# A sparse graph layer on one core: the first group's second tile of records found on chip, products turned, classes by limits

## The chip, the cores and the metric

The kernel runs on one core of a Trainium2 chip. Its time is the device time of one execution in microseconds (us), from the first to the last instruction with what the launch adds around it. The engines named below are TensorE (PE in the profile, its weight loads PEld), VectorE (DVE), ScalarE (ACT), GpSimd (POOL) and SyncE (SP), which issues the plain DMAs. Each engine works through its own queue in order.

## The reference

Sixteen graphs of 1024 nodes, 64 channels per node, and a dense adjacency matrix drawn so that a node has some four neighbours in the mean, very unevenly spread (the first nodes have many). Two layers follow each other. The first is a mean over neighbours; the second takes, per node and channel, quartiles over a thinned-out list of neighbours, and sends the result through a small network:

```python
# layer 0
h = jnp.maximum(_layernorm(x, axis=-1), 0.0)
deg = jnp.clip(jnp.sum(A, axis=2, keepdims=True), 1.0, None)
x = x + jnp.matmul(A / deg, h)
# layer 1, on h = relu(layernorm(x))
nb = (adj_ > 0) & (~eye)[None]
m = nb.sum(-1)
rank = jnp.cumsum(nb, axis=-1) - 1
skip = jnp.where(m > 10, (m + 1) // 2, 1)
removed = nb & do_dil[..., None] & ((rank + 1) % skip[..., None] == 0)
rem = removed | jnp.swapaxes(removed, 1, 2)
adj_d = jnp.where(rem, 0.0, adj_)
agg = 0.25 * q25 + 0.5 * q50 + 0.25 * q75      # over the valid neighbours, per channel
y = relu((h + agg) @ W1 + b1) @ W2 + b2
x = x + y * mask
```

## The kernel before, in words

The kernel replaces the dense second layer by lists. It has two stretches that overlap.

**Per graph** (16 times). SyncE loads the adjacency matrix in four pieces of 256 rows (tile `at`). For each 128 rows ScalarE writes the signs (`sg`) and, as an accumulated sum, the number of entries above zero (`total`); VectorE multiplies the signs by a descending ramp (`keyed`) and takes the top 8 of each of four interleaved segments (`listing`, 512 eight-way maxima in all), so that a node's neighbours are a record of up to 32 numbers, with the node's number and its mask as entries 33 and 34. TensorE transposes the blocks (`transposes`), ScalarE copies them to `att`, and `products` multiplies them by the normalized features `h0` with a column of ones, so that the sum over neighbours and the degree come out together. In the old form `h0` is the stationary operand and 512 columns of `att` move; the result has channels in its rows, so ScalarE copies it (`msg`) and TensorE transposes it back in four pieces. `channels` normalizes again and stores 1024 rows of 66 numbers to the group's table in DRAM (`tab`).

`endings` then sorts the graph's nodes by degree. It gives each node a class: the number of entries found, capped at 16, and above that one more for each of the limits 19, 22, 29, 39, 59, 79. A one-hot of 23 classes (`hot`), two matmuls against constants, and a running sum give each node its place `to` in the group's sorted order. GpSimd then scatters the node's row (table row, residual and record) to its place in DRAM (`srt`), by eight indirect DMAs a graph.

**Per group** (four groups of four graphs). The sorted nodes of a group fill 32 tiles of 128. Tile 0 holds the longest lists and is handled at the end as "long lists". Tile 1 has up to 15 neighbours, the rest fewer. `group` loads the records from `srt` (first tiles 0 and 1 alone as `recs0`, then all 32 as `recs`); for tile 0 it fetches the nodes' whole adjacency rows (`fetched`, an indirect DMA of 128 rows of 4 KB) and counts which entry the thinning takes out (`counted`); for tile 1 it does so from the list itself. The numbers of the removed neighbours (`drop`) are scattered into the group's table by two indirect DMAs, after which the neighbours' rows can be gathered: a `Job` per class of list length issues one indirect DMA per neighbour place and tile (`places`), sorts on VectorE with a network of minima and maxima, weighs on VectorE, sums and multiplies on TensorE, and scatters `y` to the output.

For group 0 the old kernel already knows tile 0's node numbers and masks before the sorted rows are in DRAM: after each of the first four graphs `hubs` compares `to` with 0 to 127 (a one-hot of 1024 elements per partition) and multiplies it with the nodes' numbers, the sum over four graphs being `hub_rows`; `begun_early` then does the fetch and the count. Tile 1's keys, both drops, and the gathers wait for `recs0` and `recs`.

**What sets the order.** All work is written as generators that a `Plan` interleaves: each `yield` names an engine and the earliest time; the plan keeps a clock per engine with a price per instruction, and always emits the entry with the lowest (time, rank). Low ranks go first: graph `b` has 10`b` plus a small number, `group` has -2000, row scatters 10`b` - 3000, the jobs 100`g` + `i`, and a job's sorting is moved ahead when GpSimd has fewer than 16 gathers ahead of it. VectorE and GpSimd keep this order exactly. Through the plan's wrapper nearly every instruction carries line 240 in the profile, so groups are told apart by their tiles. In the plan, an f32 matmul was priced so:

```python
time = 0.1 + math.prod(out.shape[1:]) * 0.88e-3
if op == "matmul" and rest[0].dtype == F32:
    time *= 2
```

The long lists' key (`long_lists`, four times) is written by the following operation, whose result is laid out in eight segments of 128:

```python
nc.vector.scalar_tensor_tensor(
    segs.rearrange("p s q -> p q s"), full.rearrange("p (q s) -> p q s", s=LSEG), 0.0,
    rev.rearrange("p (q s) -> p q s", s=LSEG), op0=OP.is_gt, op1=OP.mult,
)
```

Of the kernel before, what the change touches and what calls it, by code (L numbers as in the profile page):

```python
# [9 lines left out]
F32 = mybir.dt.float32  # L10
# [8 lines left out]
P = 128  # L19
# [9 lines left out]
NSEG = 4  # L29
STEPS = (16, 19, 22, 29, 39, 59, 79)  # L30
CLS = 15 + len(STEPS) + 1

# [15 lines left out]
MOST = 8  # L48

# [196 lines left out]
class Plan:  # L246
# [36 lines left out]
    def note(self, engine, op, args, kwargs):  # L283
# [22 lines left out]
        elif engine == "PE":  # L306
            time = 0.1 + math.prod(out.shape[1:]) * 0.88e-3
            if op == "matmul" and rest[0].dtype == F32:
                time *= 2
# [76 lines left out]
def list_path(ctx, tc, x, adj, nodemask, w1, b1, w2, b2, out, go):  # L386
# [36 lines left out]
    nc.vector.tensor_scalar(off_diag, diff, 0.0, None, op0=OP.not_equal)  # L423
    earlier = consts.tile([P, P], BF, name="earlier")
# [8 lines left out]
    nc.vector.tensor_copy(col_f, col)  # L433
    zero = consts.tile([P, 1], BF, name="zero")
# [6 lines left out]
    cls_i = grp.tile([P, N], I32, name="gat_rows", bufs=1)[:, :CLS * NT]  # L441
    cls_i = cls_i.rearrange("p (c t) -> p c t", t=NT)
    nc.gpsimd.iota(cls_i, pattern=[[-1, CLS], [0, NT]], base=CLS - 1, channel_multiplier=0)
    cls = consts.tile([P, CLS, NT], F32, name="cls")
    nc.vector.tensor_copy(cls, cls_i)
# [267 lines left out]
    def products(pool, now):  # L713


        for b, st in enumerate(batch):
            now[0] = b
            for hf in range(2):
                yield "PE", lambda: INF if st["copied"][hf] < 2 * BPH else max(
                    at(st["att"][hf]), known(st, "h0"), room("ps_small", 3)  # L720
                )
                po = new(ps_s, [P, HALF], F32, "ps_small", 3, users=1)
                for q in range(NT):
                    if q and q % 2 == 0:
                        yield "PE", always
                    nc.tensor.matmul(
                        po[:C + 1, :], st["h0"][:, q, :], st["att"][hf][:, q, :],
                        start=(q == 0), stop=(q == NT - 1),
                    )
                free(st["att"][hf])  # L730
                free(st["h0"])
                yield "ACT", lambda: max(at(po), room("msg", 2))
                msg = new(pool, [C + 1, HALF], F32, "msg", 2)
                nc.scalar.copy(msg, po[:C + 1, :])
                free(po)
                yield "PE", lambda: max(at(msg), room("ps_small", 3))
                pb = new(ps_s, [P, HALF], F32, "ps_small", 3, users=1)
                sums = pb[:, :BPH * (C + 1)].rearrange("p (k c) -> p k c", c=C + 1)
                for k in range(BPH):
                    nc.tensor.transpose(  # L740
                        sums[:, k, :], msg[:, k * P:(k + 1) * P], ident[:C + 1, :C + 1]
                    )
# [15 lines left out]
    def channels(pool, now):  # L758

        for b, st in enumerate(batch):  # L760
# [9 lines left out]
            st["normed"] = True  # L770

    def endings(pool, now):

        first = lambda rank: rank - 3000
        for b, st in enumerate(batch):
# [6 lines left out]
            for t in range(NT):  # L782
# [6 lines left out]
            found = new(pool, [P, NT, 8 * NSEG], BF, "found", 1)  # L789
            nc.vector.tensor_scalar(found, rec, 0.0, None, op0=OP.is_gt)  # L790
            d = new(tiny, [P, NT], F32, "d", 2)
            nc.vector.tensor_reduce(d, found, AX.X, OP.add)
            full = new(tiny, [P, NT], F32, "full", 2)
            nc.vector.tensor_reduce(
                full, found.rearrange("p t (s e) -> p t s e", e=8)[:, :, :, 7], AX.X, OP.max
            )
            nc.vector.scalar_tensor_tensor(d, full, float(STEPS[0]), d, op0=OP.mult, op1=OP.max)
            nc.vector.tensor_scalar(d, d, float(STEPS[0]), None, op0=OP.min)
            for s in STEPS[1:]:
                nc.vector.scalar_tensor_tensor(d, total, float(s), d, op0=OP.is_gt, op1=OP.add)  # L800
            free(rec)
            free(total)
            hot = new(tiny, [P, CLS, NT], BF, "hot", 2)
            nc.vector.tensor_tensor(
                hot, cls, d.unsqueeze(1).to_broadcast([P, CLS, NT]), OP.is_equal
            )
# [33 lines left out]
            if g == 0:  # L840
                plan.add(hubs(b, to), 10 * b + 8)
# [28 lines left out]
    class Job:  # L870
# [11 lines left out]
        def run(self):  # L882
# [14 lines left out]
            if short:  # L897
# [3 lines left out]
                if "S" not in share:  # L901
                    S = share["S"] = new(
                        pool, [P, mine_of(share), C], F32, "S", 4, users=share["users"]
                    )
                    nc.sync.dma_start(S, share["rows"][:, :, :C])
# [23 lines left out]
            yield from self.sort()  # L929

# [296 lines left out]
    hub_rows = consts.tile([P, 2], F32, name="hub_rows")  # L1227
    early = {}

    def hubs(b, to):  # L1230

        tof = new(tiny, [P, NT], F32, "tof", 2)
        yield "DVE", lambda: max(at(to), room("gfound", 1))
        nc.vector.tensor_copy(tof, to)
        where = new(grp, [P, N], HF, "gfound", 1).rearrange("p (t k) -> p t k", t=NT)
        nc.vector.tensor_tensor(
            where, col_f[:, :P].unsqueeze(1).to_broadcast([P, NT, P]),
            tof.unsqueeze(2).to_broadcast([P, NT, P]), OP.is_equal,
        )
        yield "PE", lambda: max(at(where), room("ps_small", 3))  # L1240
        ph = new(ps_s, [P, HALF], F32, "ps_small", 3, users=1)
        for t in range(NT):
            nc.tensor.matmul(
                ph[:, :2], where[:, t, :], marks[:, b, t, :], start=(t == 0), stop=(t == NT - 1)
            )
        yield "DVE", lambda: at(ph) + SLACK
        if b:
            nc.vector.tensor_tensor(hub_rows, hub_rows, ph[:, :2], OP.add)
        else:
            nc.vector.tensor_copy(hub_rows, ph[:, :2])  # L1250
# [628 lines left out]
```

## Time and profile before

| | us |
|---|---|
| median of 3 runs (lowest, highest) | 1414.26 (1410.16, 1416.34) |
| the profiled execution's own time | 1414.18 |
| its span, first to last instruction | 1412.4 |
| VectorE busy | 1228.7 (87%) |
| GpSimd busy | 963.8 (68%) |
| TensorE busy | 738.8 (52%) |
| ScalarE busy | 557.6 (39%) |
| GpSimd's first gather of neighbours / last gather | 194.84 / 1360.5 |
| mean granted TensorE clock | 0.711 |

A line in order of time reads: start, duration (both us), engine, line, operation, result <- operands with shapes, count, and in brackets the idle time of the engine just before it with what ended it; "issue" is idle time in which nothing that the profile shows was waited for. A line of a group by shape reads: result <- operands, shapes, count | total busy us, mean ns of one | idle us before, and what ended it. In the table of 40 slices each digit is the busy share of a slice in tenths. In the matmul rows an f32 product counts twice, since it is done in two passes, and a transpose once.

### The profile page before, as it was taken

How to read it: one execution, taken by the hardware profiler on the slowest of the kernel's cores; microseconds unless marked ns; L12 is line 12 of the kernel's file. 1: busy time of each engine (PE TensorE's matmuls, PEld its weight loads, DVE VectorE, ACT ScalarE, POOL GpSimd, SP SyncE). 2: the span in 40 equal slices, each digit the busy share in tenths (PEclk: the TensorE clock that was granted, in tenths of full speed). 3: DMA queues.
4: the chain of work that ended last, by engine and by line, in shares of the span. 5: the costliest groups of instructions: out<-in, count | busy, mean ns of one | idle time of the engine just before them, and what ended most of it. 6: DMA issues, size and time to landing. Idle time of an engine off the chain costs nothing.

```text
span 1412.4 us, 14420 instructions
## 1 busy us (share of the span) xinstructions
PE 738.8 (52%) x3203; PEld 458.2 (32%) x3203; DVE 1228.7 (87%) x4150; ACT 557.6 (39%) x1603; POOL 963.8 (68%) x1115
## 2 busy tenths in 40 slices
PE   4878726376677657839856652002002232337685
PEld 2434413243443335425442331001001121226455
DVE  6999898999888898998999668886998899998985
ACT  6889763765554356865653520000000110001010
POOL 0042347777775787776778877775877777787764
PEclk9999868687787868968966865555555555557566
DMA  5464582443444245545541324211111111111110
GB/s 174 156 195 163 182 228 76 133 154 90 124 107 136 69 119 170 150 142 148 158 125 46 85 46 84 73 44 46 32 25 24 25 34 26 25 28 40 25 25 16
DMA packets 133834, 132.31 MB, mean 94 GB/s; under 512 B 99444, under 2 KB 102132, under 8 KB 133620
## 3 DMA queue, kind: packets, MB, share of 16 engines
q1 hardware_dynamic: 102220, 91.13, 21.8%
q0 software_dynamic: 31520, 40.19, 11.7%
q8 instruction: 27, 0.44, 0.1%
q14 instruction: 67, 0.55, 0.1%
HBM read 111.76 MB, written 23.61 MB: 96 GB/s over the span
## 4 chain that ended last, share of the span: by engine, by line
DVE 46%; POOL 18%; issue 10%; PE 10%; DMA 9%; ACT 6%; SPq 0%; DVEq 0%; POOLq 0%; ACTq 0%
POOL places L240 14%; DVE places L240 8%; DVE rec L240 6%; DVE other L240 5%; PE ps_small L240 5%; PE pt L240 5%; DVE lplaces L240 4%; DVE sg L240 2%; DMA at<-in_adj_dram 2%; DMA places<-tab,idx 2%; DVE l0other L240 2%; ACT sg L240 2%; POOL srt L240 2%; DVE prod L240 2%; DVE lkey L240 1%
## 5 line engine op out<-in xcount | busy, mean ns | idle before, releaser
L240 POOL DMA_INDIRECT places<-tab,idx x372 | 375.8, 1010 | 121.2 <-issue 104.2
L240 PE MATMUL pt<-ident,prod 128*128 128x128 f32 (+1 forms) x736 | 152.2, 367 | 385.8 <-DVE prod L240 330.9
L240 PE MATMUL ps_small<-att,h 128*65 128x512 f32 x512 | 261.7, 662 | 77.3 <-ACT h L240 55.9
L240 PEld LDWEIGHTS pt<-ident,prod 128*128 128x128 f32 (+1 forms) x736 | 126.0, 252 | 418.0 <-DVE prod L240 248.6
L240 POOL DMA_INDIRECT srt<-row,to x128 | 131.6, 1028 | 140.0 <-ACT row L240 118.9
L240 PE MATMUL pt<-ident,at 128*128 128x128 f32 x1024 | 164.0, 304 | 72.0 <-ACT att L240 52.7
L240 DVE MAX8 rec<-sg 128x8 f16<-128x256 f16 x512 | 180.2, 414 | 4.4
L240 ACT ACTIVATE sg<-at 128x1024 f16<-128x1024 f32 x128 | 134.8, 1054 | 102.0 <-DMA at<-in_adj_dram 65.6
L240 POOL DMA_INDIRECT lplaces<-whole,lidx x125 | 146.8, 1174 | 38.1 <-issue 36.9
L240 ACT COPY ot<-pt 128x128 f32<-128x128 f32 (+3 forms) x56 | 22.4, 400 | 377.4 <-PE pt L240 377.2
L240 PEld LDWEIGHTS pt<-ident,at 128*128 128x128 f32 x1024 | 125.7, 155 | 113.9 <-ACT att L240 77.6
L240 POOL DMA_INDIRECT places<-tab,last_idx x124 | 135.0, 1089 | 37.8 <-issue 35.0
L240 ACT COPY att<-pt 128x512 f32<-128x512 f32 x256 | 140.7, 584 | 26.8 <-PE pt L240 25.3
L240 PEld LDWEIGHTS ps_small<-att,h 128*65 128x65 f32 x512 | 76.1, 155 | 220.9 <-issue 125.0
L240 POOL DMA_INDIRECT out_dram<-y,nodes_i x93 | 95.7, 1029 | 20.6 <-issue 12.7
L240 DVE TENSOR_TENSOR sg<-sg,keyed 128x1024 f16<-128x1024 f16 x128 | 87.4, 682 | 15.6 <-ACT sg L240 15.6
L240 ACT ACTIVATE wu<-wu 128x39 f32<-128x39 f32 (+9 forms) x40 | 9.4, 235 | 152.0 <-DVE wu L240 152.0
L240 PE MATMUL ps_small<-ot,w_sb 128*128 128x128 f32 (+3 forms) x112 | 52.0, 554 | 30.8 <-DVE base L240 11.9
L240 DVE TENSOR_TENSOR places<-places,other 128x128 f32<-128x128 f32 (+6 forms) x160 | 56.4, 355 | 3.4
L240 PE MATMUL ps_small<-w_sb,hid 128*128 128x64 f32 x256 | 50.1, 332 | 1.9 <-ACT hid L240 1.6
L240 DVE TENSOR_TENSOR places<-other,places 128x128 f32<-128x128 f32 (+5 forms) x136 | 48.8, 366 | 1.7
L240 DVE TENSOR_TENSOR other<-places 128x256 f32<-128x256 f32 (+4 forms) x124 | 48.1, 388 | 1.9
(292 smaller groups left out, 1600.7 us busy)
## 6 DMA issues: line engine op xcount, KB each, us to landing
at<-in_adj_dram SPq DMA_DIRECT2D x64, 1024.0 KB, 5.6
places<-tab,idx POOLq DMA_INDIRECT x372
whole<-tab SPq DMA_DIRECT2D x4, 1057.0 KB
tab<-row SPq DMA_DIRECT2D x16, 264.0 KB, 3.8
xt<-in_x_dram SPq DMA_DIRECT2D x16, 256.0 KB, 6.7
S<-srt SPq DMA_DIRECT2D x12, 192.0 KB, 2.6
y<-srt SPq DMA_DIRECT2D x12, 192.0 KB, 2.7
srt<-row,to POOLq DMA_INDIRECT x128
```

Of the source, the lines that this page charges most:

```text
L240: ins = getattr(self._engine, op)(*args, **kwargs)
```

## The change

1. `endings`: the class is found by comparing `total` (raised to 17 where a segment's eighth entry is in use) with 24 constant limits at once (`above`), and the one-hot is the difference of neighbouring results. The reduction of the found entries and the six operations for the limits go, as do the class constants made by GpSimd.
2. `products`: a 128x128 block of `att` is the stationary operand and the 65 columns of `h0` move: 32 products per half instead of 8, each 65 columns wide, with nodes in the rows of the result. The copy to `msg` and the four transposes go. A product may begin when the blocks of its 128 rows are there. The plan's price of small f32 products becomes 0.22.
3. `hubs`, `begun_early`, `group`: the one-hot covers 256 places and is 16-bit throughout; it multiplies the whole 34-number records for tile 1 (`marked`, a 16-bit copy made by ScalarE) as well as number and mask for tile 0. So for group 0 the keys of tile 1, both drops and the first job (15 gathers) are made from `hub_rows`, without `recs0`. These parts get ranks of -3000. The drops wait until the four graphs' table rows are stored. The load of the first job's own rows waits on SyncE until the fourth graph's rows are scattered (`own_rows`).
4. `long_lists`: the key is written in order and read in strides; `rev` is laid out the same way.

```diff
-STEPS = (16, 19, 22, 29, 39, 59, 79)
-CLS = 15 + len(STEPS) + 1
+STEPS = (*range(1, 17), 19, 22, 29, 39, 59, 79)
+CLS = len(STEPS) + 1
...
-                time *= 2
+                time = 0.22 if out.shape[-1] <= C_MAX else 2 * time
...
+    limits = consts.tile([P, CLS + 1, NT], F32, name="limits")
+    for c, limit in enumerate((HUGE, *reversed(STEPS), -HUGE)):
+        nc.vector.memset(limits[:, c, :], float(limit))
...
+                for k in range(BPH):
+                    yield "PE", lambda: INF if st["copied"][hf] < 2 * k + 2 else max(
+                        at(st["att"][hf]), known(st, "h0"), 0.0 if k else room("ps_small", 3)
                     )
...
+                    for q in range(NT):
+                        nc.tensor.matmul(
+                            sums[:, k, :], st["att"][hf][:, q, k * P:(k + 1) * P],
+                            st["h0"][:, q, :], start=(q == 0), stop=(q == NT - 1),
+                        )
...
-                msg = new(pool, [C + 1, HALF], F32, "msg", 2)
-                nc.scalar.copy(msg, po[:C + 1, :])
...
-            for s in STEPS[1:]:
-                nc.vector.scalar_tensor_tensor(d, total, float(s), d, op0=OP.is_gt, op1=OP.add)
+            nc.vector.tensor_scalar(full, full, 0.0, 17.0, op0=OP.is_gt, op1=OP.mult)
+            nc.vector.tensor_tensor(total, total, full, OP.max)
...
+            nc.vector.tensor_tensor(
+                above, total.unsqueeze(1).to_broadcast([P, CLS + 1, NT]), limits, OP.is_gt
+            )
...
+            nc.vector.tensor_tensor(hot, above[:, 1:, :], above[:, :CLS, :], OP.subtract)
...
-                plan.add(hubs(b, to), 10 * b + 8)
+                plan.add(hubs(pool, b, to, row), 10 * b - 3000)
...
+        marked = new(pool, [P, NT, REC], HF, "marked", 1, users=1)
+        nc.scalar.copy(marked, row[:, :, R0:])
...
         nc.vector.tensor_tensor(
-            where, col_f[:, :P].unsqueeze(1).to_broadcast([P, NT, P]),
-            tof.unsqueeze(2).to_broadcast([P, NT, P]), OP.is_equal,
+            where, col_h.unsqueeze(1).to_broadcast([P, NT, 2 * P]),
+            tof.unsqueeze(2).to_broadcast([P, NT, 2 * P]), OP.is_equal,
         )
...
-            plan.add(begun_early(), 10 * GROUPS[0] - 1)
+            plan.add(begun_early(), -3000)
...
+        full = yield from fetched(0, mine)
+        yield "DVE", always
...
+        headed(keys, first[:, :8 * NSEG], first[:, REC - 1:], drop)
...
+        yield from counted(full, mine, drop)
+        yield "POOL", lambda: max(at(drop), *(st.get("stored", INF) for st in batch[:GROUPS[0]]))
+        dropped(0, didx, drop)
...
+        job = first_job(0, keys, idx, hub_rows[:, REC - 2:REC - 1], hub_rows[:, REC - 1:REC], nodes_i)
+        plan.add(job.run(), 0)
...
             nc.vector.scalar_tensor_tensor(
-                segs.rearrange("p s q -> p q s"), full.rearrange("p (q s) -> p q s", s=LSEG), 0.0,
-                rev.rearrange("p (q s) -> p q s", s=LSEG), op0=OP.is_gt, op1=OP.mult,
+                segs, full.rearrange("p (q s) -> p s q", s=LSEG), 0.0,
+                rev.rearrange("p (s q) -> p s q", s=LSEG), op0=OP.is_gt, op1=OP.mult,
             )
```

`headed` and `dropped` hold, unchanged in their operations, what `group` did in place for tile 1's keys and for the two drops; the other three groups call them there.

## The prediction

> **What bounds the kernel now.** I read first the page's totals and its 40 slices (35.3 us each), then GpSimd in order of time with the idle time before each instruction, then VectorE's groups by shape, TensorE in order of time, and last the end of the chain.
>
> ```profile
> span 1412.4 us, 14420 instructions
> PE 738.8 (52%) x3203; PEld 458.2 (32%) x3203; DVE 1228.7 (87%) x4150; ACT 557.6 (39%) x1603; POOL 963.8 (68%) x1115
> DVE  6999898999888898998999668886998899998985
> POOL 0042347777775787776778877775877777787764
> ```
>
> VectorE is nearly full throughout. GpSimd's 7s are full too: each indirect DMA holds it 0.94 us and leaves 0.30 us that nothing ends ("issue"), 1.25 us a gather. Its real waits are few:
>
> ```profile
> 171.52 0.96 POOL L240 DMA_INDIRECT srt<-row,to  x1 [0.19 <-issue]
> 185.69 0.96 POOL L240 DMA_INDIRECT tab<-drop,didx  x1 [13.22 <-DVE didx L240]
> ...
> 189.52 0.96 POOL L240 DMA_INDIRECT tab<-drop,didx  x1 [2.76 <-DVE keys L240]
> 194.84 0.97 POOL L240 DMA_INDIRECT places<-tab,idx  x1 [4.36 <-DVE nodes L240]
> 196.11 1.05 POOL L240 DMA_INDIRECT places<-tab,idx  x1 [0.30 <-issue]
> ...
> 430.39 0.96 POOL L240 DMA_INDIRECT tab<-drop,didx  x1 [10.05 <-DVE base L240]
> ...
> 436.64 0.97 POOL L240 DMA_INDIRECT places<-tab,idx  x1 [4.03 <-DVE nodes L240]
> ```
>
> From graph 3's last row scatter (171.52) to the first gather (194.84) it idles 20.3 us (13.22 + 2.76 + 4.36). After that only four waits matter: 14.1 us when group 1 begins (430 to 437), 6.0 us at 648 (group 2's fetch), 1.5 us at 865, 9.3 us at 985 (first long lists). So GpSimd sets the pace from 195 on, and VectorE sets when each group is ready. After the last gather (1360.5) VectorE still works off long lists until 1397, then
>
> ```profile
> 1397.09 6.20 PE pt L240 x32
> ```
>
> and a fixed close of 15 us: the end is VectorE's backlog. A gain reaches the end only if both engines get it.
>
> **What the Trainium skill says.** "SBUF — State Buffer", section "Door 1: The DMA port swizzle", the note on cachelines: an access that leaves its 16-byte line pays a penalty. The trace agrees: the reduction over `base` reads 4-byte elements 32 bytes apart and takes 484 ns for 184, where contiguous reductions (512 in 670 ns, 256 in 420 ns) give about 0.98 ns each on a fixed 0.17 us; so 1.71 ns an element. "VectorE: DVE Perf Modes", "What auto-detection actually checks": the two-per-cycle mode of a two-tensor operation wants every tensor 16-bit with step 1. `sg` times `keyed` agrees (1024 in 682 ns); no row shows a broadcast operand. "TensorE: Matmul & The Clock Gate", "LDWEIGHTS": a load takes columns divided by 1.2, 107 ns for 128. The rows below agree.
>
> ```profile
> L240 DVE SCALAR_TENSOR_TENSOR lkey<-gat_rows,rev 128x1024 f16<-128x1024 f32 x4 | 18.8, 4700 | 0.1
> L240 DVE SCALAR_TENSOR_TENSOR d<-total,d 128x8 f32<-128x8 f32 x96 | 16.0, 167 | 3.3
> L240 DVE TENSOR_REDUCE pos<-base 128x8 f32<-128x184 f32 x16 | 7.8, 484 | 0.6
> L240 DVE TENSOR_REDUCE d<-found 128x8 f32<-128x256 bf16 x16 | 6.7, 420 | 0.5
> L240 DVE TENSOR_TENSOR hot<-cls,d 128x184 bf16<-128x184 f32 x16 | 5.6, 352 | 0.5
> L240 DVE TENSOR_TENSOR gfound<-col_f,tof 128x1024 f16<-128x1024 f32 x4 | 4.9, 1226 | 0.1
> L240 DVE TENSOR_SCALAR found<-rec 128x256 bf16<-128x256 f16 x16 | 3.6, 225 | 0.0
> ```
>
> **The change, part by part.**
>
> *Classes by limits* (`endings`, 16 graphs). In order of time the old run stands from `found` at 175.69 to the next work at 178.40: 2.71 us. New: one reduction of 32 (0.24), two operations on 8 elements (0.20 each), `above` of 192 (0.37 from `hot`'s row plus 0.03), `hot` of 184 all bf16 (0.25 to 0.35; I take 0.30). Sum 1.31, so -1.40 x 16 = -22.4 us of VectorE. The new class count is 23 as before, so the matmuls and the scan stay.
>
> *Long-list key* (4). It read in order and wrote 2-byte elements 256 bytes apart: 4.70 us. Now it reads 32 bytes apart and writes in order: 0.17 + 1024 x 1.71 ns = 1.92 us. Bounds: 1.28 (the row of the same operation, contiguous) and 4.70 (reads no better than writes). I take 1.92: -2.78 x 4 = -11.1; `rev` once pays +1.2.
>
> *Hub products* (`hubs`, 4). The one-hot doubles to 2048. Bounds 1.27 us (0.10 + 2048 x 0.57 ns, the 16-bit rate) and 2.30 (twice 1.226 less a fixed 0.15). `tof` is broadcast with step 0, so by the page above 2.30: +1.07 x 4 = +4.3 us. Index columns and bases written twice, wider sums: +1.0. ScalarE's copy of `marked`, 272 elements, about 0.4 us x 4, is covered by ScalarE's idle time; without cover it costs 0.4 a graph.
>
> *Products turned* (32 halves).
>
> ```profile
> 85.18 7.03 PE L240 MATMUL ps_small<-att,h 128*65 128x512 f32 x16
> 92.05 1.04 PE L240 MATMUL pt<-ident,at 128*128 128x128 f32 x8
> 92.92 0.42 PE L240 MATMUL ps_small<-ident,msg 65*128 65x65 f32 x4
> 93.36 1.14 PE L240 MATMUL pt<-ident,at 128*128 128x128 f32 x8
> ...
> 1099.51 1.00 PE L240 MATMUL ps_small<-w_sb,hid 128*128 128x64 f32 x8
> 1100.35 0.65 PE L240 MATMUL ps_small<-ot,w_sb 128*128 128x256 f32 x2
> ```
>
> Before, a half is 16 passes (two per f32 product) in 6.87 us and 4 transposes in 0.44: 7.31. Now it is 64 passes with a new 128-column load and 65 columns each. The nearest rows: `hid` by `w_sb`, 8 passes in 0.84 (0.105 each, at half clock), and the transposes of `at`, 8 in 0.87 (0.11). 64 x 0.11 = 7.0 us, so -0.3. Bounds per pass 0.056 (65 columns at the old rate, 0.43/512 x 65) and 0.25 (load 155 ns and pass in a row). ScalarE loses the 32 `msg` copies (0.575 each, -18.4 us) and each half one hop between engines; ScalarE isn't the bound (39%), so I count 0.
>
> *First group's start.* The list fetch, hub sums and drop get first rank. Graph 3's `to` is at 142.65; its one-hot waited until 144.96, `hub_rows` stood at 152.03, the fetch went at 155.37, landed at 162.3, and counting ended at 170.4. At once: one-hot 142.0 to 144.5, products and margin to 147, fetch 148, landed 155, counted 163. Tile 1's keys and drops (4.2 us of VectorE, formerly at 185 to 189.5) fit in the fetch, whose stall of 3.4 us (with the listings queued behind it) goes. The drops then wait for graph 3's table store: its rows are done at 160.9 and the store lands in 3.8 us, 165. On GpSimd from 161: 8 scatters x 1.27 and 2 drops x 1.27 = 12.7, so the first gather at about 174, 21 us earlier; the 15 gathers of the first job (19 us) cover until the record load and its searches are done (about 190). The scatters queue behind the two drops: if the store is late they slip with it, and nothing else does. SP: one 34 KB load goes, the first rows' load moves behind graph 3 and has 20 us before the sort wants it. Bounds: 0 to 22 us.
>
> *Constants.* 24 small memsets for one cast and a GpSimd iota: under 1 us, inside VectorE's 8.3 us wait at the start.
>
> **The sum.** VectorE: -22.4 - 11.1 + 1.2 + 4.3 + 1.0 - 3.4 = -30.4. But GpSimd has to follow, stage by stage. Group 1 needs graph 7: VectorE gains 8 x 1.40 - 5.3 + 3.4 = 9.3 by then, plus part of the 4.8 us it waited at 216 for the first gathers: 12. GpSimd, 21 ahead, gives 9 back as a longer wait at 430. Group 2: VectorE 17 ahead, GpSimd 12 plus 5 of the 6.0 wait = 17. Group 3: VectorE 23, GpSimd 17 plus 1.5 = 18.5. Long lists: three keys are made by 985 and shorten the 9.3 us wait by some 4.5: 23. The close keeps its length. 1412.4 - 23 = 1389.4 span; the profiled execution has 1.8 us around its span (1414.18), and the median of the runs (1414.26) is the same: 1391. The written-out order changes everywhere, since its cost for small products does; for that I allow 8 us either way.
>
> **Rivals.**
> - *A, forecast* (0.55): 1391, its own range 1380 to 1401.
> - *B, the gain is stuck behind GpSimd* (0.14): graph 7 comes only 8 x 1.40 - 5.3 = 6 us earlier, later waits give 2 more, the rest is spent waiting at group starts. 1406. For it: GpSimd's gapless 1.25 us. Against it: its own waits lie on VectorE.
> - *C, VectorE pays in full* (0.12): -30.4 and the 4.8 us wait: 1379. For it: the last 36 us are VectorE's alone. Against it: 23 slices where GpSimd is full.
> - *D, TensorE becomes the bound* (0.10, slower). In the first four graphs (`to` every 31 us) TensorE is busy 85% from 50 to 150 us, so about 5.3 us free per graph. A graph's products may then grow from 14.6 to 19.9 us, 128 passes of 0.155: from there it decides. At 0.25 a pass, 12 us x 4 = 48 later at the first gather, less the 23 gained and about 8 recovered in the 430 wait: 1431. Against it: the two rows at 0.11.
> - *E, the early start doesn't come* (0.09): the table store or the fetch lands late and the first gather stays near 190. VectorE's part alone, through the same waits (6, 11.5, 13, 17.5): 1397.
>
> **How the numbers follow.** Half a per cent, 7 us, is about what can be told from no change. Faster: A 0.54, B 0.08, C 0.12, E 0.08 = 0.82. Same: A 0.01, B 0.06, E 0.01 = 0.08. Slower: D, 0.10. The range 1370 to 1411 leaves out D and the end of C.
>
> **What would show it.** `above` and `hot` near 0.37 and 0.3 us, `lkey` at 1.9, the one-hot at 2.3, product passes 0.11 us apart, the first gather near 174, the wait before group 1's drop near 20 us, last gather 20 us earlier. Wrong if the first gather is later than 190, a pass is over 0.155, or GpSimd shows new waits over 10 us after 440.

## The result, and the profile after

The changed kernel takes 1474.31 us (median of 4 runs, 1470.43 to 1477.48) beside 1412.49 for the kernel before on the same chip: a ratio of 1.043, 95% interval 1.039 to 1.048. It is slower, where 1391 was forecast, and above the range of 1370 to 1411. The profiled execution has a span of 1469.1 us, 56.7 more than before.

The page's totals and slices (36.7 us each) of the changed kernel:

```profile
span 1469.1 us, 17198 instructions
PE 792.9 (54%) x4643; PEld 690.3 (47%) x4643; DVE 1204.6 (82%) x4065; ACT 542.3 (37%) x1575; POOL 951.5 (65%) x1120
DVE  5777889799686998679968855896999699999895
PEclk8868885758669567588667585555555556566577
```

VectorE was to lose work, and did: 1228.7 to 1204.6 us busy. But its first five slices, 6, 9, 9, 9, 8 before, are now 5, 7, 7, 7, 8: it has less to do and waits more. TensorE is busy for 54 us more. GpSimd in order of time, where the first gather was forecast at 174:

```profile
188.72 0.97 POOL L241 DMA_INDIRECT gat_rows<-in_adj_dram,hnodes_i  x1 [17.58 <-PE pt L241]
...
205.41 0.96 POOL L241 DMA_INDIRECT tab<-drop,didx  x1 [3.23 <-DVE full L241]
...
210.43 0.97 POOL L241 DMA_INDIRECT places<-tab,idx  x1 [2.81 <-DMA tab<-drop,didx]
```

The list fetch goes at 188.7, not 148, and the first gather at 210.4, not 174 (194.8 before; later than 190 was named as a sign of being wrong). Most of this comes before the early start: graph 3's row positions (`to`) stand only at 168 us, where they stood at 143. The graphs themselves have become slower, 37 us apart and not 31 (`to` at 56, 97, 136, 168; before 49, 81, 111, 143). The rest is lost between `to` and the fetch, 20.5 us where the forecast had 6 (148 less 142): graph 3's one-hot is done at 172.8, but its hub product stands behind turned products and transposes in TensorE's order until 181.2,

```profile
177.66 1.90 PE L241 MATMUL ps_small<-h,att 128*128 128x65 f32 x16
...
181.17 0.35 PE L241 MATMUL ps_small<-marked,gat_rows 128*128 128x34 f16 x8
```

and the index columns stand in VectorE's order behind a listing that waits 3 us for its signs, until 187.2. From group 3's fetch to the end it takes about the same (549 us after, 547 before): the loss is made in the graph phase, and `to` of the sixteenth graph stands at 900 us, before at 830.

VectorE's groups by shape, for the pieces that were priced:

```profile
L241 DVE TENSOR_TENSOR gat_rows<-col_h,tof 128x2048 f16<-128x2048 f16 x4 | 9.2, 2292 | 0.1
L241 DVE SCALAR_TENSOR_TENSOR lkey<-gat_rows,rev 128x1024 f16<-128x1024 f32 x4 | 7.9, 1987 | 0.1
L241 DVE TENSOR_TENSOR above<-total,limits 128x192 bf16<-128x192 f32 x16 | 5.7, 358 | 0.5
L241 DVE TENSOR_TENSOR hot<-above 128x184 bf16<-128x184 bf16 x16 | 4.2, 261 | 0.6
```

2.29, 1.99, 0.36 and 0.26 us, against 2.30, 1.92, 0.37 and 0.30 in the forecast. VectorE's part was priced rightly. The products were not. TensorE's group of products before and after,

```profile
L240 PE MATMUL ps_small<-att,h 128*65 128x512 f32 x512 | 261.7, 662 | 77.3 <-ACT h L240 55.9 <-DVE row L240 11.0 <-ACT att L240 5.4
L241 PE MATMUL ps_small<-h,att 128*128 128x65 f32 x2048 | 316.9, 327 | 97.5 <-ACT h L241 83.4 <-DVE row L241 6.2 <-ACT att L241 5.0
```

and after in order of time (start, length, shape of the output, number of passes):

```profile
64.63 7.34 PE L241 MATMUL ps_small<-h,att 128*128 128x65 f32 x64
...
72.25 7.26 PE L241 MATMUL ps_small<-h,att 128*128 128x65 f32 x64
...
91.06 6.98 PE L241 MATMUL ps_small<-h,att 128*128 128x65 f32 x32
```

316.9 us for 2048 passes is 0.155 a pass. But hardly a pass takes 0.155: 64 passes in 7.3 us are 0.11 each, 32 in 6.98 are 0.22. Here are the two stretches (TensorE busy, instructions, granted clock, DMA share, GB/s):

```profile
91.00:107.00 16.00, 16.00 (x78) 0.50 0.33 117
64.00:80.00 16.00, 16.00 (x159) 1.00 0.20 67
```

The granted clock is 1.00 from 64 to 80 us and 0.50 from 91 to 107, and TensorE has no gap in either. Whole, the turned products take 317 us for the old 262.

What that does to the other engines can be read in ScalarE's waits: here one in order of time, in the stretch shown above,

```profile
72.50 0.58 ACT L241 COPY att<-pt 128x512 f32<-128x512 f32 x1 [6.23 <-PE pt L241]
```

and then the sums of two waits, of the changed kernel (us in total, times, longest)

```profile
ACT att L241 <- PE pt L241: 95.4, 85, 8.2
DVE sg L241 <- ACT sg L241: 65.4, 16, 8.8
```

and of the kernel before:

```profile
ACT att L240 <- PE pt L240: 25.3, 57, 2.0
DVE sg L240 <- ACT sg L240: 15.6, 5, 7.3
```

This is the chain, as the traces have it. ScalarE copies transposed blocks; the next four transposes stand behind the products in TensorE's order; so ScalarE waits (6.23 us there). The sign passes that VectorE needs stand in ScalarE's order behind the copies; so VectorE waits for `sg`, 50 us more than before. From 20 to 140 us, busy time of each engine, before:

```profile
20.00:140.00 120.00, 97.47 (x432) 48.46 (x432) 112.67 (x404) 103.69 (x263) 22.69 (x42) 0.94 0.50 166
```

and after (the columns are PE, PEld, DVE, ACT, POOL, then granted clock, DMA share and GB/s):

```profile
20.00:140.00 120.00, 91.79 (x623) 85.46 (x622) 89.63 (x303) 79.63 (x193) 18.56 (x32) 0.76 0.43 131
```

VectorE and ScalarE do 23 and 24 us less work in the same 120 us. TensorE is busy for 92 of 120: it isn't full either. The three wait for each other in turn.

### The profile page after: what moved, and what is told of

Read it like the earlier page. It is cut to its first block, busy times and chain, and to the rows that moved or that the text cites. A ratio compares the mean times of both kernels' runs of the same rounds, so it can differ in the third digit from the quotient of the medians.

```text
span 1469.1 us, 17198 instructions
## 1 busy us (share of the span) xinstructions
PE 792.9 (54%) x4643; PEld 690.3 (47%) x4643; DVE 1204.6 (82%) x4065; ACT 542.3 (37%) x1575; POOL 951.5 (65%) x1120
## 5 line engine op out<-in xcount | busy, mean ns | idle before, releaser
L241 PE MATMUL ps_small<-h,att 128*128 128x65 f32 x2048 | 316.9, 327 | 97.5 <-ACT h L241 83.4
L241 PEld LDWEIGHTS ps_small<-h,att 128*128 128x128 f32 x2048 | 312.8, 244 | 101.9 <-ACT h L241 85.0
L241 PE MATMUL pt<-ident,prod 128*128 128x128 f32 (+1 forms) x736 | 167.3, 393 | 337.2 <-DVE prod L241 270.6
L241 PEld LDWEIGHTS pt<-ident,prod 128*128 128x128 f32 (+1 forms) x736 | 136.2, 272 | 366.2 <-DVE prod L241 206.2
L241 PE MATMUL pt<-ident,at 128*128 128x128 f32 x1024 | 169.7, 309 | 78.3 <-ACT att L241 31.4
L241 PEld LDWEIGHTS pt<-ident,at 128*128 128x128 f32 x1024 | 131.8, 161 | 107.7 <-ACT att L241 52.8
L241 POOL DMA_INDIRECT lplaces<-whole,lidx x125 | 134.3, 1074 | 38.1 <-issue 36.6
L241 ACT ACTIVATE hid<-ps_small,b_sb 128x128 f32<-128x128 f32 (+2 forms) x56 | 28.2, 503 | 87.1 <-PE ps_small L241 86.9
```

The lines of the kernel that those rows point to most:

```text
L241: ins = getattr(self._engine, op)(*args, **kwargs)
```

## The experiments

Two theories. T: the turned products take more TensorE time than the old ones and slow the graph phase. S: the loss lies elsewhere, in the order: the early start, or the order written out with a new price for small products. All times stand beside the kernel before on the same chip, 1412 to 1413 us in the first eight runs, and the ratios and intervals are to that.

**Undo the turn, do the turn alone, do the early start alone, do classes and key alone.** The edits are the parts of the diff. With the old products back, the second `msg` buffer no longer fits beside `marked`, so the first and the third have one.

> The changed kernel with its products turned back (h0 stationary, 512 columns of att moving, the copy to msg and the transposes; msg has one buffer in place of two for want of SBUF), all else changed. Theory T1, the turned products cost it all (64 short passes a half, 0.21 us each where the granted clock is half and 0.11 where it is full, against 16 long ones at 0.44): the rest of the change is worth what was forecast, 1391 us, 1375 to 1405. Theory T2, the first-rank hub work and the early job put VectorE's order wrong, so that features come late to TensorE (its waits for h are 83 us against 56): still 1440 to 1470.

> The kernel before with the products turned and the plan's price of small f32 products at 0.22, nothing else. T1: 1480 us, 1455 to 1500, since the losses of the turn come without the gains of the rest; product passes at 0.105 and 0.21 us as in the changed kernel, first gather 10 to 25 us later than 195. T2: 1400 to 1415.

> The kernel before with only the first group's second tile from the hub products, its early fetch, drops and first job (msg with one buffer for want of SBUF). T1: the first gather near 174 us instead of 195, part of it lost again in the wait before group 1, together 1395 to 1405 us. T2: 1440 to 1470, with longer waits of TensorE for h.

> The kernel before with only the classes by limits and the long lists' key written in order. Both theories: VectorE's busy time falls by 32 us (1.40 x 16 + 2.78 x 4 - 1.2), as each wait of GpSimd on VectorE shortens the time goes to 1397 us, 1385 to 1407.

Measured: without the turn 1426.1 (ratio 1.009, interval 1.007 to 1.011); the turn alone 1534.0 (1.084, 1.079 to 1.089); the early start alone 1446.4 (1.024, 1.021 to 1.026); classes and key alone 1411.2 (0.999, 0.998 to 1.001).

The turn costs, alone and in the change; alone it costs more than the 1455 to 1500 that theory T allowed. But it isn't all: without it the kernel should have been near 1391, and was at 1426, in neither theory's range; and the early start, forecast at -21 us for the first gather, cost 34 alone. GpSimd in order of time without the turn:

```profile
174.96 1.28 POOL L241 DMA_INDIRECT tab<-drop,didx  x1 [20.25 <-DVE rec L241]
...
187.18 0.94 POOL L241 DMA_INDIRECT places<-tab,idx  x1 [0.30 <-issue]
188.43 1.00 POOL L241 DMA_INDIRECT srt<-row,to  x1 [0.30 <-issue]
```

The fetch went at 153.7 and the first gather at 179.2, some 5 us after the forecast and 16 before the old kernel's. But GpSimd stood idle for 20 us at the first drop, with graph 3's eight scatters and seven gathers behind it, and the scatters went at 188 to 198 (161 to 172 before). The sorted records of group 0 can only be loaded behind them, so VectorE stood still next:

```profile
205.39 0.20 DVE L241 MAX8 keys<-recs 128x8 f32<-128x32 f32 x1 [9.34 <-DMA recs<-srt]
```

The run with classes and key shows a second thing: VectorE has 30 us less to do (1198.3 busy) and the time doesn't move. What was saved turns into waiting, the longest at 416 us. The load queue of SyncE, then GpSimd, then VectorE, each in order of time:

```profile
376.92 0.37 SPq L240 DMA_DIRECT2D tab<-row  x1
402.78 0.88 SPq L240 DMA_DIRECT2D recs<-srt  x2
403.71 2.72 SPq L240 DMA_DIRECT2D S<-srt  x1
406.61 2.90 SPq L240 DMA_DIRECT2D y<-srt  x2
409.60 0.45 SPq L240 DMA_DIRECT2D at<-in_adj_dram  x1
...
388.10 1.96 POOL L240 DMA_INDIRECT places<-tab,idx  x1 [0.30 <-issue]
390.36 1.27 POOL L240 DMA_INDIRECT srt<-row,to  x1 [0.30 <-ACT att L240]
...
415.91 0.69 DVE L240 TENSOR_TENSOR sg<-sg,keyed 128x1024 f16<-128x1024 f16 x1 [17.18 <-ACT sg L240]
```

The load of group 1's records stands in the queue for 25.4 us until graph 7's row scatters are done, and these begin at 390.4, after an unbroken row of gathers on GpSimd. The loads of `S` and `y` and then the adjacency rows stand behind the records in the queue (the wait of `y` itself, for a scatter to the output, is 1.7 us). ScalarE's sign pass waits for the adjacency rows until 414.7, and VectorE for the signs. So here too scatters came late behind gathers. That chain is read from one trace; no run took it away.

**The drops behind the scatters, a filler for the clock, 16-bit operands before, the old price.** The edits, the first on the kernel without the turn, the second and fourth on the changed kernel, the third on the kernel before:

```diff
-        yield "POOL", lambda: max(at(drop), *(st.get("stored", INF) for st in batch[:GROUPS[0]]))
+        yield "POOL", lambda: INF if progress["batches"] < GROUPS[0] else max(
+            at(drop), *(st.get("stored", INF) for st in batch[:GROUPS[0]])
+        )
```

```diff
                         sums = pb[:, :BPH * (C + 1)].rearrange("p (k c) -> p k c", c=C + 1)
+                        for _ in range(16):
+                            nc.tensor.matmul(
+                                pb[:, 260:], off_diag, col_h[:, :252], start=True, stop=True
+                            )
...
+            if op == "matmul" and out.shape[-1] == 252:
+                time = 0.11
```

```diff
-            h0 = new(pool, [P, NT, C + 1], F32, "h0", 2, users=2)
+            h0 = new(pool, [P, NT, C + 1], HF, "h0", 2, users=2)
...
-                        st["att"][hf] = new(pool, [P, NT, HALF], F32, "att", 2, users=1)
+                        st["att"][hf] = new(pool, [P, NT, HALF], HF, "att", 2, users=1)
```

```diff
-                time = 0.22 if out.shape[-1] <= C_MAX else 2 * time
+                time *= 2
```

> The kernel of the run without the turned products (1426), with one edit: GpSimd's two drops of group 0 wait until graph 3's row scatters are issued. Theory 'slipped scatters' (the early start costs because the drops, with 20 us of idle GpSimd ahead of them and seven gathers behind them, pushed the scatters from 161-172 to 188-198, so that the records of group 0 are late): the scatters are back at 161-172, the first gather is at 176-182, the 9.3 us that VectorE waited for the records near 205 fall under 2 us, and the time falls to 1405-1414. Rival 'sort ahead of graphs' (the early first job puts its sort before graphs 4 to 7 in the order, and their transposes and listings slip): the scatters move, but graph 5, 6 and 7 have their row positions at 252, 319 and 381 as before this edit (245, 303 and 370 in the kernel before the change), and the time stays at 1420-1430.

> The changed kernel (1474), with sixteen idle 16-bit passes of 252 columns ahead of each half's turned products, written to a spare part of the same PSUM bank; they add 1.7 us of TensorE per half at the full clock and 3.4 at half. Theory 'clock' (a turned pass is 0.105 us at the full granted clock and 0.21 at half, and a burst of 65-column passes that starts at half clock stays there): the filler brings the clock up, the mean of the 2048 turned passes falls from 0.155 to 0.105-0.125, the granted clock between 91 and 107 us is near 1.0 rather than 0.5, and the time falls to 1435-1460. Rival 'the load is slow in itself' (whatever the clock): the mean stays at 0.15 or more, and the time rises to 1475-1500, since TensorE has 54 to 109 us more work.

> The kernel before the change, with the two operands of the graph products (the transposed adjacency and the normed rows) stored in 16 bits, so that each product is one pass and not two; the sums are rounded differently. A half's products should fall from 6.9 us to 1.7-3.5, so TensorE loses 110-165 us. Theory 'TensorE bounds the graph phase' (the premise of the rival that has TensorE as the bound, at 5 us free per graph): the first four graphs have their row positions every 27 us or less rather than every 31, and the time is 1385 or less. Rival 'the chain of ScalarE, the load queue and VectorE bounds it, TensorE has slack': the spacing stays at 30-31 us and the time is 1400-1415.

> The changed kernel with the one edit of the order's cost for small products undone: a turned product counts 0.31 us again and not 0.22. The chip's work is the same, only the order written out differs. Theory 'the passes themselves' (0.155 us on average, 0.31 per product, so TensorE has 95 us more to do in the graph phase): the time stays within 10 us of 1474. Rival 'the order was planned with a price that is too low, and engines wait in the wrong order': the time falls by 20 us or more, to 1455 or less, and ScalarE's waits for the transposed blocks fall from 95 us to under 60.

*Drops behind the scatters:* 1388.9 (1388.3 to 1391.7), ratio 0.984, interval 0.982 to 0.987. GpSimd in order of time:

```profile
168.32 0.99 POOL L241 DMA_INDIRECT srt<-row,to  x1 [13.52 <-ACT row L241]
...
179.16 1.22 POOL L241 DMA_INDIRECT tab<-drop,didx  x1 [0.30 <-DVE rec L241]
...
183.95 0.97 POOL L241 DMA_INDIRECT places<-tab,idx  x1 [2.31 <-DMA tab<-drop,didx]
```

The scatters begin at 168.3 (not quite 161, since the rows themselves come then), the drops follow without a wait, and VectorE's wait for the records is gone. The first gather goes 5 us later than without this edit, and the kernel is 37 us faster. So the order was the loss of the early start. The theory of slipped scatters holds in its mechanism; its range, 1405 to 1414, was too cautious. Of the rival, a sort that pushes back the next graphs, little is left: `to` of graphs 5, 6 and 7, at 252, 319 and 381 without this edit, stands at 243, 297 and 375 (245, 303 and 370 in the kernel before). In the changed kernel the slip wasn't at work: there the scatters were ahead of the drops already (190 to 200, drops at 205), and the same edit leaves every instruction of that kernel as it is. So the kernel of this run is the changed kernel but for the turn, what the turn does to the written order, and one `msg` buffer: the turn costs 85 us (1474 less 1389), not the 48 that undoing it alone showed.

*Filler:* 1470.9, ratio 1.042 (1.039 to 1.045). TensorE's group of the turned products:

```profile
L241 PE MATMUL ps_small<-h,att 128*128 128x65 f32 x2048 | 281.9, 301 | 66.2 <-ACT h L241 61.7 <-ACT att L241 4.5
```

The mean is 0.138 a pass, down from 0.155. As before, the passes are of two kinds, 0.11 where the clock is up and 0.21 where it is at half, and fewer are of the slow kind (by the spacing of their starts a fifth, in the changed kernel over a third): a pass is slow where the clock is down. Neither theory's numbers were met, though. The mean missed 0.105 to 0.125 because some bursts still start cold. From 91 to 107 us the clock is 0.90 here, up from 0.50, but the filler isn't shown to have done that: it had risen under transposes some 3 us before the first filler pass there,

```profile
94.23 1.14 PE L241 MATMUL pt<-ident,at 128*128 128x128 f32 x8 [0.20 <-ACT att L241]
...
97.68 1.88 PE L241 MATMUL ps_small<-col_h,off_diag 128*128 128x252 f16 x16
99.40 7.26 PE L241 MATMUL ps_small<-h,att 128*128 128x65 f32 x64
```

and the filler adds 74.8 us of TensorE where the passes gain 35. Nor can the time of this run be laid on that alone. In the order written for it graph 3's scatters slipped again: they go at 219 us, behind both drops (203.5) and seven gathers, with 28 us of idle GpSimd ahead of the drops. Without the turn that cost 37 us. What a filler is worth with the scatters held in front was not run.

*16-bit operands in the kernel before:* 1401.9, ratio 0.993 (0.991 to 0.996). The products fall from 262 to 93 us and the time by 10. `to` stays at 49, 82, 112, 144: the kernel before is hardly held up by its products.

*Old price:* 1491.3, ratio 1.057 (1.051 to 1.063). The time moved by 17 us, upwards, where theory T allowed 10 and the rival, that the low price made the order bad, wanted 20 or more downwards. But the total doesn't decide between them, since the scatters slipped in this order too, behind 15 gathers:

```profile
209.04 0.98 POOL L241 DMA_INDIRECT tab<-drop,didx  x1 [31.43 <-DMA tab<-row]
...
234.99 0.94 POOL L241 DMA_INDIRECT places<-tab,idx  x1 [0.30 <-issue]
236.23 0.99 POOL L241 DMA_INDIRECT srt<-row,to  x1 [0.30 <-issue]
```

What speaks against the rival is the graph phase ahead of that: the fourth `to` stands at 167 us with the old price and at 168 with the new, and the passes are no faster (0.161). ScalarE's waits for the transposed blocks are 111.5 us, not under 60 as the rival had it. The mean of a pass differs with the order (0.161 here, 0.173 with the turn alone).

**Passes or order?** Four further edits: one burst (each of a half's four products waits for all eight blocks), the early start alone with the drops behind the scatters, and 16-bit operands both without the turn and with it. The short one:

```diff
-                    yield "PE", lambda: INF if st["copied"][hf] < 2 * k + 2 else max(
+                    yield "PE", lambda: INF if st["copied"][hf] < 2 * BPH else max(
```

> The changed kernel (1474) with one edit: all four products of a half wait for the half's eight transposed blocks, as they did before the change, and not each for its own two; so 64 turned passes stand in one burst and not in four of 16 with transposes between. Theory 'bursts too short' (the clock falls to half because the products are cut into pieces of 16 passes): the mean of the turned passes falls from 0.155 to 0.13 or less, and the time to 1440-1462. Rival 'it is the 65 columns' (a pass that streams so few columns doesn't bring the clock up however long the burst is): the mean stays at 0.145 or more, and the time at 1465-1500, later if anything, since the first products start later.

> The kernel before the change with its early start alone (1446 as it stands in the change), and the one edit that GpSimd's two drops wait until graph 3's scatters are issued. Theory 'the order of drops and scatters': the loss goes, the first gather is at 180-188, and the time is 1395-1415; what the run with scatters first gained over this one (1389) is then VectorE's saving on classes and key. Rival 'the early first job displaces graphs 4 to 7 when VectorE has not been relieved': graph 7's row positions stay at 400 or later and the time at 1425-1446.

> The kernel of the run with scatters first (1389, products not turned), with the two operands of the graph products stored in 16 bits, so that each product is one pass; the sums are rounded differently. If TensorE has slack there, as the same edit to the kernel before showed (1402 against 1412), it gives 3 to 12 us: 1377-1387. If the mended start made TensorE the limit, it gives 20 or more: under 1370.

> The changed kernel (its own order puts the drops behind the scatters already; that order is also fixed here) with turned products whose operands are stored in 16 bits: 32 passes a half and not 64; the sums are rounded differently. Theory 'TensorE's time for the passes is what the turn costs': with half the passes, and weight loads of half the width, the cost goes, and the time is within 1% of the unturned 16-bit kernel of this call (1370-1395). Rival 'the turn costs through its order and its waits (products asked for block by block, a PSUM buffer held longer, ScalarE's copies later)': the time stays at 1415 or more.

> The changed kernel with turned products in 16 bits: 32 passes a half and not 64, each with a narrower weight load; the sums are rounded differently. Theory 'TensorE's time for the passes is what the turn costs': within 1% of the unturned 16-bit kernel of this call, so about 1370-1395. Rival 'the turn costs through its order and its waits': 1415 or more.

> The kernel with scatters first (1389, products not turned) with the operands of the graph products in 16 bits; the sums are rounded differently. TensorE has slack there: 1377-1387. If the mended start made TensorE the limit: under 1370.

> The kernel before with the early start alone and the drops behind graph 3's scatters. Theory 'the order of drops and scatters was the loss of the early start (1446)': 1395-1415, first gather at 180-188; the rest of the way to 1389 is VectorE's savings. Rival 'the early first job displaces graphs 4 to 7': 1425-1446, graph 7's row positions at 400 or later.

> The changed kernel with all four products of a half behind the half's eight transposed blocks, 64 turned passes in one burst. Theory 'bursts too short': the mean of a turned pass falls from 0.155 to 0.13 or less, and the time to 1440-1462. Rival 'the 65 columns': the mean stays at 0.145 or more and the time at 1465-1500.

> The changed kernel with turned products in 16 bits (the sums are rounded differently). If TensorE's time for the passes is what the turn costs, it is within 1% of the other kernel of this call: 1375-1400 where the kernel before takes 1412, or a ratio of 0.966-0.969 where it takes some 1820. If the order and the waits of turning cost: 2% or more above the other kernel.

> The kernel with products not turned, in 32 bits, and the drops behind graph 3's scatters (0.984 of the kernel before in its own call), as the partner of the turned 16-bit kernel. Where the kernel before takes 1412: 1386-1392. Where it takes some 1820: 0.965-0.985 of it, 0.965 if TensorE has slack there too, 0.985 if it doesn't.

The ten runs met three other chips, on which the kernel before takes 1815 to 1824 us. VectorE's and GpSimd's operations last as long there as elsewhere (an eight-way maximum 414 ns on both, a gather 1.0 us), but from about 170 us on TensorE and ScalarE show idle stretches of up to 25 us and more that the profile gives to nothing ("issue") or to nothing it can name ("remote"); what causes them is open. The absolute forecasts for these runs are therefore neither met nor missed. Only ratios within a chip count, and the first 150 us of the traces, which look as on the other chips. Two forecasts were given as ratios for such chips: 0.966 to 0.969 for the last run turned in 16 bits, which took 0.971, and 0.965 to 0.985 for scatters first, which took 1.010 and missed.

| kernel | ratio to before (chips in order) | interval |
|---|---|---|
| turned, 16 bits | 0.966, 0.969, 0.971 | each ±0.005 to 0.008 |
| not turned, 16 bits | 0.967, 0.965 | ±0.005, ±0.004 |
| not turned, 32 bits, scatters first | 1.010 (third chip) | 1.006 to 1.014 |
| turned, 32 bits, one burst | 1.057, 1.062 | ±0.006 |
| early start alone, scatters first | 0.991, 0.996 | ±0.004, ±0.003 |

Turned or not, in 16 bits the time is the same within half a per cent, on two chips, although the turned kernel keeps what turning does to the work's structure: products asked for block by block, a PSUM buffer held through four products, no `msg`. (The order itself is written anew, as a 16-bit product counts 0.16 us in the plan and not 0.22.) The first graphs say it in time, on all chips (when `to` of the fourth graph is written, us):

| kernel | fourth `to` |
|---|---|
| before; without the turn; with scatters first | 143; 142; 142 (144 on a later chip) |
| early start alone; with scatters first | 145; 147, 150 |
| not turned, 16 bits | 146, 146 |
| turned, 16 bits | 150 to 151 |
| turned, 32 bits: changed; one burst; filler; old price; turn alone | 168; 169; 163; 167; 181 |

Only the turned 32-bit kernels are late by 20 us or more. Their passes do it; the two rows of 16 bits are only some 4 us apart. The pass itself in 16 bits, turned (1024 of them, from the trace of the second of these chips):

```profile
L241 PE MATMUL ps_small<-h,att 128*128 128x65 f16 x1024 | 78.4, 227 | 132.8 <-issue 108.5 <-ACT att L241 8.6 <-ACT h L241 8.1
```

is 0.077 us, and there are half as many: 78 us in all for 317.

*One burst:* 0.172 and 0.173 us a pass, and `to` at 55, 97, 135, 169. So the bursts were not too short. The turn alone has the clearest stretch, beside a burst of the old products that starts cold:

```profile
102.69 27.55 PE L241 MATMUL ps_small<-h,att 128*128 128x65 f32 x128
25.18 9.48 PE L240 MATMUL ps_small<-att,h 128*65 128x512 f32 x16 [3.51 <-ACT att L240]
```

128 turned passes without a gap stay at a clock of 0.50 for 27.5 us. The 16 old ones begin at 0.85 us a pass and are at 0.43 from the seventh on. Whether it is the 65 columns or the weight load of each pass that leaves the clock down, no run separates. The times of the one-burst runs (1.057, 1.062) are not to be set beside the changed kernel's 1.043: graph 3's scatters slipped there too (215 us, behind seven gathers).

*Early start alone, mended:* the loss of 2.4% is gone (0.991 and 0.996). That fits the order as the cause, but the forecast 1395 to 1415 couldn't be tried where it was meant.

*Scatters first* is 1.6% faster than before on the chip with 1412 and 1.0% slower on a chip with some 1820: it beats the kernel before on the first kind only. Not turned in 16 bits is 3.3 and 3.5% faster there; it was not run on a chip of the first kind, and it rounds the sums differently.

## Why the prediction was wrong, point by point

**Classes, key, hub one-hot: right.** 27.0 us of VectorE's busy time were to go, 24.1 went. The two pages of the Trainium skill carried this. The key pays the penalty for leaving its 16-byte line ("SBUF — State Buffer", "Door 1") at the rate worked out from `pos` and `base` (1.99 us for 1.92), and the 16-bit rate stayed away from the broadcast one-hot (2.29 us for 2.30), as "VectorE: DVE Perf Modes" has it under "What auto-detection actually checks": its operand doesn't have step 1.

**"-30.4" as time: wrong, and not only because of the turn.** Classes and key alone took 30 us off VectorE's busy time and nothing off the total. VectorE's nearly full slices were taken for a bound; they were one member of a ring in which SyncE's queue, ScalarE and TensorE take turns. I asked which engine is busiest, and should have asked which waits end last in the graph phase: ScalarE's for the adjacency rows (65.6 us before the change), VectorE's for `sg` behind them.

**"64 x 0.11 = 7.0 us per half": the step that failed.** It measured 9.9 (317 over 32), 0.155 a pass. The row taken as a price was "`hid` by `w_sb`, 8 passes in 0.84 (0.105 each, at half clock)". The clock there was in fact 1.00; it is 0.50 only up to 1098 us (same columns as in the two stretches above):

```profile
1099.00:1101.00 2.00, 2.00 (x15) 1.00 0.07 18
1086.00:1098.00 12.00, 11.27 (x34) 0.50 0.13 25
```

So the price at full clock was read as the price at half clock, and nothing was kept for half. The estimate of 107 ns for a 128-column load, from the Trainium skill's formula ("TensorE: Matmul & The Clock Gate", "LDWEIGHTS"), fits a pass of these 32-bit operands at full clock (0.105 to 0.11); at half a pass took 0.21 to 0.22. The same page, in Part 1, says that the array's clock is released by activity. In these traces the turned passes, without a gap for 27.5 us, did not release it. The old 512-column passes did: about half of their bursts (15 of 32) start cold too, at 0.85 us a pass, and come to 0.43 within the burst. The old side was mis-sized as well, too low: 6.87 a half for the products, where the mean was 8.2 (262 over 32), since those cold starts count in it. So a half's work on TensorE grew by about 1.3 us (9.9 for 8.2 and 0.44 of transposes), where -0.3 was forecast.

**"About 5.3 us free per graph": wrong.** The rival with TensorE as the bound was the right one, and its threshold, 128 passes of 0.155 a graph, is the mean that was measured. But at that mean it was to begin, not to cost 26 us in four graphs. TensorE's idle time between 50 and 150 us, 15 us, was for 11.5 us waits for ScalarE's copies, inside the ring, and no reserve: a longer product pushes the next transposes, and with them ScalarE and VectorE. The delay of 26 us at the fourth graph, with 0.155 a pass, lies between the forecast's 0 and the rival's 48 with 0.25 a pass.

**"If the store is late they slip with it, and nothing else does": wrong,** and hidden in the changed kernel. Without the turn the scatters stood behind the drops, as the prediction saw, and more slipped: gathers went ahead of them, then the record load, then VectorE, and with it the graphs. The forecast -21 us at the first gather became +34 at the end with the early start alone.

**The sum.** With the turn taken out and the drops behind the scatters it is 1389, where 1391 was said. That agreement is luck in good part: group 1's and 2's fetches came 5 and 9 us earlier (12 and 17 forecast), group 3's 35 (18.5 forecast), and the last stage then took 560 us and not 547. And on a chip with 1820 us it is a loss.

## What to carry to other kernels

Price a TensorE pass at both clocks, look up the granted clock of the very stretch the row comes from, and ask whether the new passes bring the clock up at all. Idle time of an engine that feeds and is fed by others in turn is no reserve: ask who stands behind the longer instruction in its queue. When a wait moves ahead of other work, hold it back until that work is issued: here one condition was worth 37 us. And where every edit has the order written anew, look for an old fault in each new order before comparing totals: here the slipped scatters came back with the filler, the old price and the one burst.

## What was not expected of the hardware

A 32-bit pass of 65 columns with its own 128-column load takes 0.105 to 0.11 us at the full granted clock and 0.21 to 0.22 at half, and 128 of them in a row, 27.5 us without a gap, stayed at half. The same turned pass with 16-bit operands took 0.077 us on average at a mean granted clock of 0.59. And the kernel before took 1412 us where it was first run and 1815 to 1824 on three other chips, with idle stretches that no recorded wait explains; the sign of one and the same kernel's difference (scatters first, 0.984 and 1.010) turned round between them.
